# The second layer's expert tiles: the last three of 39 put behind a test of the tile count

## The chip, the cores and the metric

The kernel runs on one core of one Trainium2 chip. The metric is the device time of one execution in microseconds (us). The core has five engines that run side by side, each with its own queue of instructions: TensorE (PE in the profile; its weight loads are PEld), VectorE (DVE), ScalarE (ACT), GpSimd (POOL) and SyncE (SP). A difference of under 0.5% (8 us) is about what a few runs of this kernel cannot tell from none.

## The reference

Two layers work on x, 4 x 512 tokens of 512 numbers in float32. Each layer adds a gated attention and then a gated mixture of experts. The part that the change touches is the mixture of experts of the second layer (`_L1_ffn_ref`), with B*S = 2048 tokens, E = 8 experts of width F = 256, and K = 2 experts for each token:

```python
h = _rmsnorm(x, rms_weight)
ht = h.reshape(-1, d)
logits = ht @ router_w
probs = jax.nn.softmax(logits, axis=-1)
topv, topi = jax.lax.top_k(probs, K)
topv = topv / jnp.sum(topv, axis=-1, keepdims=True)
...
g = jnp.einsum('td,edf->tef', ht, w_gate)
u = jnp.einsum('td,edf->tef', ht, w_up)
eo = jnp.einsum('tef,efd->ted', jax.nn.silu(g) * u, w_down)
moe = jnp.einsum('te,ted->td', w_dense, eo)
sh = jax.nn.silu(ht @ sw_gate) * (ht @ sw_up) @ sw_down
```

`w_dense` holds the two weights of a token in the columns of its two experts. The result, `moe + sh`, is scaled by tanh(g_ffn[1]) and added to x. The inputs are drawn with a fixed seed, so the routing is the same in each run.

## The kernel before

The kernel goes through its stages in order: attention of layer 0, experts of layer 0, attention of layer 1, experts of layer 1. The change is in the last.

**Routing of layer 1** (lines 1806 to 1898). The router's logits give each token its two experts. The tokens of each expert are put one behind the other into *slots*, and each expert's slots begin at a new tile of 128. `cnt` is the number of tiles of each expert (its tokens plus 127, shifted right by 7), and `ends` is the running sum over the experts, so its last column is the number of tiles in use. How many that is depends on the data; at most it is `SLOTS` = (2 * 2048 + 8 * 127) // 128 = 39, and the kernel always works 39 tiles. `idx` holds for each tile the 128 rows of the table to fetch; unused slots point at 128 padding rows behind the 2048 tokens. `owner` is the expert of each tile (for tiles beyond the last in use it is the last expert), and `owners` the same as a one-hot. These are small VectorE operations; between them `advance(besides)` sets the shared expert of the last batch, on TensorE, VectorE and SP.

**The tiles** (`slot_tiles`, line 361, called from line 1923 for layer 1). One tile is:

- `fetch`: POOL starts an indirect DMA that gathers 128 rows of `table1` into `got` (line 368). `got` has depth + 1 = 6 buffers, and `fetch` runs five tiles ahead.
- `turn`: TensorE transposes `got` (4 products, line 379); VectorE scales it into `h_t` (line 383) and makes the tile's weight `wt` (lines 1916, 1917).
- `up`: 8 products with the gate and up weights of the tile's expert (line 397), then Silu on ScalarE (line 406) and a product on VectorE (line 407). The expert's number is read from `owner` into a register of TensorE (line 1907).
- `turn_mid`: 2 transposes (line 413) and a copy on ScalarE (line 415).
- `down`: 4 products with the down weights (line 421), a scaled copy on ScalarE (line 425), and an indirect DMA from POOL that adds the 128 rows to `out` (line 426). Such a scatter waits for the one before it to land.

The loop interleaves these as a pipeline: for each j it issues the fetch of tile j + 5, the middle turn of j - 1, the turn of j + 1, gate and up of j, and down of j - 1. All eight experts' weights are in SBUF before. The order on PE, DVE, ACT and POOL is the one written (`manual_schedule`); no planner moves instructions here.

**The end.** After the last scatter every engine runs a drain and a barrier (line 1997 in the profile). POOL's drain begins behind its last scatter.

**A branch that is there already** (line 1070). In layer 0 each expert has five tiles that always run; more of them, up to sixteen for each expert, stand in a `tc.If` that tests the largest token count, `most`. Each engine loads the value into a register, compares, and either runs the body or jumps behind it, where it updates the semaphores that the body would have updated.

Of the kernel before, what the change touches and what calls it, by code (L numbers as in the profile page):

```python
# [10 lines left out]
FP = mybir.dt.float32  # L11
BF = mybir.dt.bfloat16
I32 = mybir.dt.int32
# [5 lines left out]
P = 128  # L19
B, S, D = 4, 512, 512  # L20
# [16 lines left out]
E1, F1 = 8, 256  # L37
# [2 lines left out]
SLOTS0 = 5  # L40

SLOTS = (2 * B * S + E1 * (P - 1)) // P


WHEN = {'keys': (-7, -6, -5, -3, -2, -1, 0, 2, 3, 4, 5, 6, 7),
# [19 lines left out]
WIDE = D + E1  # L65
# [10 lines left out]
def kernel(  # L76
# [32 lines left out]
    nc = tc.nc  # L109
# [13 lines left out]
    def bank(name):  # L123
        return phase[0].tile([P, 512], FP, tag="bank", bufs=phase[1], name=name)

    def two_banks(name):
        return phase[0].tile([P, 2, 512], FP, tag="two", bufs=2, name=name)
# [31 lines left out]
    table1 = tc.dram_tile([ROWS, WIDE], FP, name="table1")  # L159
# [201 lines left out]
    def slot_tiles(sp, tiles, table, total, width, rms, besides=lambda j: None, depth=3):  # L361

        nf = width // P

        def fetch(j):
            t = tiles[j]
            t.got = sp.tile([P, WIDE], FP, tag="got", bufs=depth + 1, name=f"got_{t.name}")
            nc.gpsimd.indirect_dma_start(  # L368
                out=t.got,
                out_offset=None,  # L370
                in_=table[:, :],
                in_offset=bass.IndirectOffsetOnAxis(ap=t.idx, axis=0),
            )

        def turn(j):
            t = tiles[j]
            tp = bank(f"gotT_{t.name}").rearrange("p (c q) -> p c q", c=NC)
            for c in range(NC):
                nc.tensor.transpose(tp[:, c, :], t.got[:, c * P : (c + 1) * P], ident)  # L379
            t.h_t = sp.tile([P, NC, P], FP, tag="h_t", bufs=2, name=f"h_t_{t.name}")  # L380
            if rms:
                w = cols_sb[:, C_RMS : C_RMS + NC].unsqueeze(2).to_broadcast([P, NC, P])
                nc.vector.tensor_tensor(t.h_t, tp, w, ALU.mult)
            else:
                nc.vector.tensor_copy(t.h_t, tp)  # L385
            t.w = t.scale(t.got[:, D:])

        def up(j):
            t = tiles[j]
            if t.gate_up is None:  # L390
                t.gate_up, t.down = t.weights()
            gu = two_banks(f"gu_{t.name}").rearrange("p k f -> p (k f)")[:, : 2 * width]
            parts = t.gate_up(0)
            n = 2 * width // len(parts)
            for k in range(len(parts)):
                for c in range(NC):
                    nc.tensor.matmul(  # L397
                        gu[:, k * n : (k + 1) * n],
                        lhsT=t.h_t[:, c, :],
                        rhs=t.gate_up(c)[k],  # L400
                        start=(c == 0),
                        stop=(c == NC - 1),
                    )
            act = sp.tile([P, width], FP, tag="slot_act", bufs=2, name=f"act_{t.name}")
            t.mid = sp.tile([P, width], FP, tag="slot_mid", bufs=2, name=f"mid_{t.name}")
            nc.scalar.activation(act, gu[:, :width], AF.Silu)  # L406
            nc.vector.tensor_tensor(t.mid, act, gu[:, width:], ALU.mult)  # L407

        def turn_mid(j):
            t = tiles[j]  # L410
            tp = bank(f"midT_{t.name}")[:, :width].rearrange("p (c q) -> p c q", c=nf)
            for f in range(nf):
                nc.tensor.transpose(tp[:, f, :], t.mid[:, f * P : (f + 1) * P], ident)  # L413
            t.mid_t = sp.tile([P, nf, P], FP, tag="mid_t", bufs=2, name=f"mid_t_{t.name}")
            nc.scalar.copy(t.mid_t, tp)  # L415

        def down(j):
            t = tiles[j]
            py = bank(f"y_{t.name}")
            for f in range(nf):  # L420
                nc.tensor.matmul(  # L421
                    py, lhsT=t.mid_t[:, f, :], rhs=t.down(f), start=(f == 0), stop=(f == nf - 1)
                )
            y = sp.tile([P, D], FP, tag="slot_y", bufs=3, name=f"y_{t.name}")
            nc.scalar.activation(y, py, AF.Copy, scale=t.w)  # L425
            nc.gpsimd.indirect_dma_start(  # L426
                out=total[:, :],
                out_offset=bass.IndirectOffsetOnAxis(ap=t.idx, axis=0),
                in_=y,
                in_offset=None,  # L430
                compute_op=ALU.add,
            )

        n = len(tiles)
        for j in range(depth):
            fetch(j)
        turn(0)
        for j in range(n + 1):
            if j + depth < n:
                fetch(j + depth)  # L440
            if j > 0:
                turn_mid(j - 1)
            if j + 1 < n:
                turn(j + 1)
            if j < n:
                up(j)
                if rms and j + 1 < n:
                    tiles[j + 1].gate_up, tiles[j + 1].down = tiles[j + 1].weights()
                besides(j)
            if j > 0:  # L450
                down(j - 1)
# [68 lines left out]
    with tc.tile_pool(name="att0", bufs=2, reuse_waits="tile") as wk:  # L520
# [9 lines left out]
        for b in range(B):  # L530
            t = Tokens()
# [246 lines left out]
        first, second = logits0(b * TB, 2), logits0(b * TB + 2, 2)  # L778
# [20 lines left out]
        def one_over(s):  # L799
# [3 lines left out]
        dist, fb, zone, rest = wide("dist"), wide("fb"), wide("zone"), wide("rest")  # L803
# [37 lines left out]
            out=table0[: B * S, D:].rearrange("(i p) e -> p i e", p=P), in_=w0  # L841
# [272 lines left out]
    for b in range(B):  # L1114
        nc.sync.dma_start(
            out=x_sb[:, b * TB : (b + 1) * TB, :],
# [8 lines left out]
    with tc.tile_pool(name="att1", bufs=1, reuse_waits="tile") as wk:  # L1125
# [8 lines left out]
        for b in range(B):  # L1134
            t = Batch()
# [486 lines left out]
        with tc.manual_schedule(engines={E.PE, E.DVE, E.Activation, E.Pool}):  # L1622
# [15 lines left out]
            for k, b in itertools.product(WHEN, range(B)):  # L1638
                first = per * b
                f = first - per  # L1640
# [23 lines left out]
                elif k == "shifted":  # L1664
                    for g in range(NC):
                        f = first + g * TB
# [79 lines left out]
    with tc.tile_pool(name="exp1", bufs=1, side="right", reuse_waits="tile") as wk:  # L1746

        wd = wk.tile([P, E1, F1 // P * D], FP, tag="wd", name="wd")
        wgu = wk.tile([P, E1, NC * 2 * F1], FP, tag="wgu", name="wgu")
        idx = wk.tile([P, SLOTS], I32, tag="idx", name="idx")  # L1750
        owner = wk.tile([P, SLOTS], I32, tag="owner", name="owner")
        owners = wk.tile([P, SLOTS, E1], FP, tag="owners", name="owners")
        shp = tc.alloc_tile_pool(name="shared1", bufs=1, side="right", reuse_waits="tile")
        shared1 = []
        for name, src in (("swg", sg1), ("swu", su1), ("swd", sd1)):
            t = shp.tile([P, *((2, 512) if name == "swd" else (4, 256))], FP, tag=name, name=name)
            load_rows(t, src)
            shared1.append(t)
        for t, src in ((wgu, wgu1), (wd, wd1)):
            for e in range(0, E1, 4):  # L1760
                nc.scalar.dma_start(
                    out=t[:, e : e + 4, :], in_=src[e : e + 4].rearrange("e p f -> p e f")
# [43 lines left out]
        with tc.tile_pool(name="route1", bufs=1, reuse_waits="tile") as rp:  # L1806
# [29 lines left out]
            ends = cnt  # L1836
            for k in range(E1.bit_length() - 1):
                t, n = rp.tile([P, E1], FP, tag="ends", bufs=2, name=f"ends{k}"), 1 << k
                nc.vector.tensor_copy(t[:, :n], ends[:, :n])
                nc.vector.tensor_tensor(t[:, n:], ends[:, n:], ends[:, : E1 - n], ALU.add)  # L1840
                ends = t
# [12 lines left out]

            pi = bank("slots")[:, : 2 * SLOTS]
            n = NT // 4
            for h in range(8):
                k, i0 = h // 4, h % 4 * n
                hot_r, hot_c = one_hots(
                    rp, row1[:, k, i0 : i0 + n], col1[:, k, i0 : i0 + n], i0, 0, SLOTS  # L1860
                )
# [9 lines left out]
                if h == 0:  # L1871
# [10 lines left out]
                        out=table1[: B * S, D:].rearrange("(i p) e -> p i e", p=P), in_=w1  # L1882
                    )
            slot_rows(rp, idx, pi)

            ge = rp.tile([P, SLOTS, E1], FP, tag="ge", name="ge")
            own = rp.tile([P, SLOTS], FP, tag="own", name="own")
# [6 lines left out]
            nc.vector.tensor_reduce(own, ge, AX.X, ALU.add)  # L1894
            nc.vector.tensor_scalar(own, own, float(E1 - 1), None, ALU.min)
            nc.vector.tensor_copy(owner, own)
            nc.vector.tensor_scalar(owners[:, :, 0:1], ge[:, :, 0:1], -1.0, 1.0, ALU.mult, ALU.add)
            nc.vector.tensor_tensor(owners[:, :, 1:], ge[:, :, :-1], ge[:, :, 1:], ALU.subtract)
            for k in range(12):
# [3 lines left out]
        def slots1(pool, j):  # L1903
            gate_up, down = (w.rearrange("p e f -> p (e f)") for w in (wgu, wd))

            def weights():
                e = nc.tensor.value_load(owner[0:1, j : j + 1], min_val=0, max_val=E1 - 1)
                n = 2 * F1
                return (
                    lambda c: (gate_up[:, bass.ds(e * (NC * n) + c * n, n)],),  # L1910
                    lambda f: down[:, bass.ds(e * (F1 // P * D) + f * D, D)],
                )

            def scale(w):
                t = pool.tile([P, E1 + 1], FP, tag="wt", bufs=4, name=f"wt_{j}")
                nc.vector.tensor_tensor(t[:, :E1], w, owners[:, j, :], ALU.mult)
                nc.vector.tensor_reduce(t[:, E1:], t[:, :E1], AX.X, ALU.add)
                return t[:, E1:]

            return Slots(f"s1_{j}", idx[:, j : j + 1], weights, scale)  # L1920

        with tc.tile_pool(name="slots1", bufs=1, reuse_waits="tile") as sp:
            slot_tiles(sp, [slots1(sp, j) for j in range(SLOTS)], table1, out, F1, True, depth=5)
    layer1.close()
    close_psum()

# [74 lines left out]
```

## Time and profile before

| what | us |
|---|---|
| three timed runs | 1603.37, 1610.71, 1612.19 |
| their median | 1610.71 |
| the profiled execution | 1603.29 |
| span of its trace, first to last instruction | 1601.5 |
| TensorE busy in the span | 1462.0 (91%) |
| layer 1's tiles: first gather issued | 1353.5 |
| first gate-and-up product | 1360.2 |
| last scatter issued | 1593.8 |
| one gather on POOL (79 of both layers) | 0.99 |
| one scatter into `out` on POOL (39) | 1.59 |
| such a scatter, issue to landing | 4.5 to 5.0 |
| granted TensorE clock, mean over the span | 0.963 |

A line of the groups reads: line, engine, operation, output <- inputs, count, busy time, mean of one in ns, and the idle time before them with what ended it. The chain is the sequence of work that ended last, followed back from the last instruction; its lines are start, length, engine and line. In a table by stretch each pair is the busy time of an engine and its number of instructions, and "PEclk" is the share of the full TensorE clock that was granted. A `q` behind an engine's name (POOLq) marks what its sequencer does, such as register loads, branches and drains.

### The profile page before, as it was taken

To read this page: it belongs to the slowest core of one execution; us is meant where nothing else is said; L and a number is where in the kernel's file an instruction comes from. 1 tells how busy PE (TensorE), PEld (TensorE's weight loads), DVE (VectorE), ACT (ScalarE), POOL (GpSimd) and SP (SyncE) were. 2 spreads that over 40 slices of the span, in tenths; PEclk is the share of its full clock that TensorE was granted. 3 is DMA by queue.
4 is the path that set the end of the run, shared out by engine and by line. 5 is a ranking of instruction groups with operands and counts; after the bars stand their busy time and mean duration, and the time that the engine had idled before them with its cause. 6 is when DMAs were issued, how large, how long until landed. Compare 5 with 4: busy or idle time off the path is not lost.

```text
span 1601.5 us, 14963 instructions
## 1 busy us (share of the span) xinstructions
PE 1462.0 (91%) x5558; PEld 648.0 (40%) x5558; DVE 643.7 (40%) x1167; ACT 474.9 (30%) x683; POOL 576.9 (36%) x454
## 2 busy tenths in 40 slices
PE   7999699999999999897878989987799987999997
PEld 3553244444444444442222332332334353445443
DVE  4755222232221211254575566556654346222221
ACT  3653111112111111333454444444434210122221
POOL 0000112213132222225458566676476411344442
PEclk9999899999999999997999999999799988999998
DMA  9414224533433422500000000000000147344453
GB/s 324 124 72 165 65 42 117 132 92 73 125 93 79 119 53 35 176 11 4 0 1 1 1 0 14 27 1 1 27 27 27 53 182 283 75 90 91 91 93 46
DMA packets 60751, 121.42 MB, mean 76 GB/s; under 512 B 10496, under 2 KB 13056, under 8 KB 59648
## 3 DMA queue, kind: packets, MB, share of 16 engines
q0 software_dynamic: 17696, 41.75, 14.1%
q1 hardware_dynamic: 35872, 64.86, 11.6%
q10 hardware_dynamic: 7104, 13.78, 2.3%
q8 instruction: 47, 0.77, 0.2%
q14 instruction: 32, 0.26, 0.1%
HBM read 81.70 MB, written 38.67 MB: 75 GB/s over the span
## 4 chain that ended last, share of the span: by engine, by line
PE 66%; DVE 7%; POOL 6%; ACT 4%; issue 3%; DMA 2%; POOLq 0%; ACTq 0%; SPq 0%; DVEq 0%
PE gu_s L397 26%; PE y_s L421 13%; DVE nm L1448 4%; PE sc L1431 4%; PE m L1431 4%; ACT pt L1481 4%; PE q L1170 2%; PE y L1170 2%; PE gotT_s L379 2%; PE gu L1170 2%; PE midT_s L413 2%; PE o L1499 2%; POOL acc L1489 2%; POOL xln L1240 1%; POOL acc L1486 1%
## 5 line engine op out<-in xcount | busy, mean ns | idle before, releaser
L368 POOL DMA_INDIRECT got_s<-table,idx x79 | 77.9, 986 | 567.5 <-ACT y_s L425 324.4
L421 PE MATMUL y_s<-wd,mid_t_s 128*128 128x512 f32 (+1 forms) x476 | 218.6, 595 | 1.6 <-ACT mid_t_s L415 1.6
L1448 DVE TENSOR_REDUCE nm<-m 128x4 f32<-128x1984 f32 x64 | 142.3, 2223 | 166.6 <-PE m L1431 166.6
L407 DVE TENSOR_TENSOR mid_s<-act_s,gu_s 128x512 f32<-128x512 f32 (+1 forms) x79 | 43.9, 555 | 393.1 <-ACT act_s L406 393.1
L1481 ACT ACTIVATE pt<-sc 128x2048 f32<-128x2048 f32 x64 | 120.2, 1878 | 191.9 <-PE sc L1431 174.3
L1489 POOL TENSOR_TENSOR acc<-acc,pt 128x2048 f32<-128x2048 f32 (+1 forms) x32 | 144.3, 4509 | 64.9 <-ACT pt L1481 64.9
L406 ACT ACTIVATE act_s<-gu_s 128x512 f32<-128x512 f32 (+1 forms) x79 | 38.9, 492 | 392.7 <-PE gu_s L397 392.6
L397 PE MATMUL gu_s<-wg,h_t_s 128*128 128x512 f32 x320 | 145.1, 596 | 0.0
L397 PE MATMUL gu_s<-wu,h_t_s 128*128 128x512 f32 x320 | 143.9, 592 | 0.0
L397 PE MATMUL gu_s<-wgu,h_t_s 128*128 x312 | 142.7, 601 | 0.0
L421 PEld LDWEIGHTS y_s<-wd,mid_t_s 128*128 128x128 f32 x476 | 89.2, 190 | 112.7 <-issue 107.5
L1431 PE MATMUL sc<-xT,k_t 32*128 32x512 f32 (+1 forms) x512 | 78.6, 685 | 34.6 <-DVE nm L1448 33.3
L1486 POOL TENSOR_TENSOR acc<-pt,pt 128x2048 f32<-128x2048 f32 x16 | 72.2, 4511 | 102.6 <-ACT pt L1481 102.6
L426 POOL DMA_INDIRECT out<-y_s,idx x39 | 61.8, 1584 | 130.2 <-ACT mid_t_s L415 122.7
L1431 PE MATMUL m<-k_t,xT 32*128 32x496 f32 x512 | 74.5, 653 | 23.8 <-ACT pt L1481 17.0
L397 PEld LDWEIGHTS gu_s<-wu,h_t_s 128*128 128x128 f32 x320 | 60.8, 190 | 76.5 <-issue 76.5
L397 PEld LDWEIGHTS gu_s<-wg,h_t_s 128*128 128x128 f32 x320 | 58.2, 192 | 58.3 <-issue 57.9
L397 PEld LDWEIGHTS gu_s<-wgu,h_t_s 128*128 128x128 f32 x312 | 57.1, 193 | 57.6 <-issue 57.6
L426 POOL DMA_INDIRECT sum<-y_s,idx x40 | 63.5, 1586 | 42.6 <-ACT y_s L425 27.1
L1499 PE MATMUL o<-pt,v 128*32 128x512 f32 (+1 forms) x512 | 72.9, 644 | 0.0
L425 ACT ACTIVATE y_s<-y_s,got_s 128x512 f32<-128x512 f32 x40 | 27.5, 687 | 122.5 <-PE y_s L421 122.5
L385 DVE COPY h_t_s<-gotT_s 128x512 f32<-128x512 f32 x40 | 27.6, 690 | 87.4 <-PE gotT_s L379 87.4
(361 smaller groups left out, 2010.9 us busy)
## 6 DMA issues: line engine op xcount, KB each, us to landing
wg<-in_wg SPq DMA_DIRECT2D x8, 1024.0 KB, 7.4
wu<-in_wu SPq DMA_DIRECT2D x8, 1024.0 KB, 7.0
wd<-in_wd SPq DMA_DIRECT2D x8, 1024.0 KB, 5.7
table<-xln SPq DMA_DIRECT2D x32, 256.0 KB, 2.0
wgu<-in_wgu ACTq DMA_DIRECT2D x2, 4096.0 KB, 15.6
ctx<-in_ctx_t SPq DMA_DIRECT2D x8, 512.0 KB, 10.4
x_sb<-in_x SPq DMA_DIRECT2D x4, 1024.0 KB, 13.8
sum<-x_sb SPq DMA_DIRECT2D x16, 256.0 KB, 2.0
```

The source lines that it names most:

```text
L368: nc.gpsimd.indirect_dma_start(out=t.got, out_offset=None, in_=table[:, :], in_offset=bass.IndirectOffsetOnAxis(ap=t.idx, axis=0),)
L397: nc.tensor.matmul(gu[:, k * n : (k + 1) * n], lhsT=t.h_t[:, c, :], rhs=t.gate_up(c)[k], start=(c == 0), stop=(c == NC - 1),)
L407: nc.vector.tensor_tensor(t.mid, act, gu[:, width:], ALU.mult)
L421: nc.tensor.matmul(py, lhsT=t.mid_t[:, f, :], rhs=t.down(f), start=(f == 0), stop=(f == nf - 1))
L426: nc.gpsimd.indirect_dma_start(out=total[:, :], out_offset=bass.IndirectOffsetOnAxis(ap=t.idx, axis=0), in_=y, in_offset=None, compute_op= ...
L1170: nc.tensor.matmul(pp, lhsT=lhs(c), rhs=w[:, c, :], start=(c == 0), stop=(c == n - 1))
L1431: nc.tensor.matmul(sc[:n, j, :width], lhsT=lhs(rs), rhs=rhs(rs), start=True, stop=True)
L1448: nc.vector.tensor_reduce(it.nm[g][:, t, :], sc[:, :, :S2], AX.X, ALU.max, negate=True)
L1481: nc.scalar.activation(it.pt[:n], sc[:n], AF.Exp)
L1486: nc.gpsimd.tensor_tensor(acc, it.pt0, it.pt, ALU.add)
L1489: nc.gpsimd.tensor_tensor(acc[:n], acc[:n], it.pt[:n], ALU.add)
L1499: nc.tensor.matmul(it.po[j * HD : (j + 1) * HD, :], lhsT=it.v[:n, c, h * HD : (h + 1) * HD], rhs=pt[:n, j, :], start=(c == 0), stop=(c == ...
```

## The change

The tiles of layer 1 are worked in two calls of `slot_tiles`: one for tiles 0 to `USUAL` - 1, with `USUAL` = (2 * 2048 + 8 * 128 // 2) // 128, and one for the tiles from there to `SLOTS` - 1. The second call stands in a `tc.If`, whose condition is that the number of tiles in use is greater than `USUAL`. That number is copied as an integer into a new tile `total` by one VectorE cast in the routing, and `values_load` reads it into a register on every engine. The second call has a pipeline of its own, with a depth of three, and begins after the first has issued its last scatter. The number of `got` buffers, which was depth + 1, is now given outright: 6 in layer 1 and 4 in layer 0, as before.

```diff
+USUAL = (2 * B * S + E1 * P // 2) // P
...
-            t.got = sp.tile([P, WIDE], FP, tag="got", bufs=depth + 1, name=f"got_{t.name}")
+            t.got = sp.tile([P, WIDE], FP, tag="got", bufs=6 if rms else 4, name=f"got_{t.name}")
...
+        total = wk.tile([P, 1], I32, tag="total", name="total")
...
             nc.vector.tensor_copy(owner, own)
+            nc.vector.tensor_copy(total, ends[:, E1 - 1 :])
             nc.vector.tensor_scalar(owners[:, :, 0:1], ge[:, :, 0:1], -1.0, 1.0, ALU.mult, ALU.add)
...
         with tc.tile_pool(name="slots1", bufs=1, reuse_waits="tile") as sp:
-            slot_tiles(sp, [slots1(sp, j) for j in range(SLOTS)], table1, out, F1, True, depth=5)
+            for first, end in ((0, USUAL), (USUAL, SLOTS)):
+                with ExitStack() as rest:
+                    if first > 0:
+                        used = nc.values_load(total[0:1, 0:1], min_val=0, max_val=SLOTS)
+                        rest.enter_context(tc.If(used > USUAL))
+                    slot_tiles(
+                        sp,
+                        [slots1(sp, j) for j in range(first, end)],
+                        table1,
+                        out,
+                        F1,
+                        True,
+                        depth=min(5, end - first),
+                    )
```

## The prediction

> **What bounds the kernel now.** I read the page first, for who is busy; then the chain that ended last, cut to the last 47 us, for how the second layer's slot tiles follow each other; then the sums by stretch, to see whether TensorE has any slack there; then the one place where the kernel already branches, for the price of a branch.
>
> The page (busy time by engine, and the chain by line):
>
> ```profile
> PE 1462.0 (91%) x5558; PEld 648.0 (40%) x5558; DVE 643.7 (40%) x1167; ACT 474.9 (30%) x683; POOL 576.9 (36%) x454
> PE gu_s L397 26%; PE y_s L421 13%; DVE nm L1448 4%; PE sc L1431 4%; PE m L1431 4%; ACT pt L1481 4%; PE q L1170 2%; PE y L1170 2%; PE gotT_s L379 2%; PE gu L1170 2%; PE midT_s L413 2%; PE o L1499 2%; POOL acc L1489 2%; POOL xln L1240 1%; POOL acc L1486 1%
> ```
>
> The chain at the end (start, length, what):
>
> ```profile
> 1571.22 3.44 PE gu_s L397 x8
> 1574.66 1.72 PE y_s L421 x4
> 1576.37 0.22 PE midT_s L413 x2
> 1576.59 0.44 PE gotT_s L379 x4
> 1577.03 3.44 PE gu_s L397 x8
> 1580.46 1.72 PE y_s L421 x4
> 1582.18 0.22 PE midT_s L413 x2
> 1582.40 3.44 PE gu_s L397 x8
> ...
> 1588.55 4.51 DMA out<-y_s,idx
> ...
> 1593.59 1.79 POOLq L1997
> ```
>
> Every tile is one turn of the same wheel on TensorE: 3.44 (gate and up) + 1.72 (down, of the tile before) + 0.22 + 0.44 (two turns) = 5.82 us; start to start, 1571.22 to 1577.03, it is 5.81. The last tile's turn is shorter (1577.03 to 1582.40, 5.37), as no tile behind it is turned. What follows is a tail: activation, product, the last y, the scatter of tile 37 landing, then that of tile 38.
>
> By stretch (length, then busy time of PE, PEld, DVE, ACT, POOL, granted clock, DMA share, GB/s), three turns in the middle and the last three full ones:
>
> ```profile
> 1397.89:1415.32 17.43, 17.43 (x55) 8.67 (x54) 4.04 (x13) 4.00 (x9) 7.73 (x7) 1.00 0.50 92
> 1565.25:1582.68 17.43, 17.43 (x54) 8.44 (x53) 4.04 (x12) 4.00 (x10) 4.67 (x3) 1.00 0.34 46
> ```
>
> TensorE is busy for all 17.43 us at full clock, no other engine for half of it. Here time goes with the number of tiles.
>
> **Does the test skip the tiles?** USUAL is (4096 + 8*64) // 128 = 36, and the body runs if the tiles in use exceed 36. The count is the sum over experts of tokens/128, rounded up. I worked out the second layer's router from the reference for the drawn inputs: 274, 456, 223, 1058, 896, 207, 769, 213 tokens, so 3+4+2+9+7+2+7+2 = 36. 36 > 36 is false: tiles 36 to 38, which hold only padding, are jumped over. It is exact: expert 4 fills seven tiles to the last row (896 = 7*128), and one more token makes 37. The closest single change of choice that does so needs a logit gap of 0.0076 to close (expert 4 third behind a second that loses no tile); the logits computed in single and in double precision differ by 5e-5 at most. With random errors of 0.003 on every logit 12 of 200 draws gave 37, with 0.001 none.
>
> **What is removed.** Tiles 36, 37, 38. The built programs' order is the same on all engines up to tile 30's scatter, but for one DVE cast and a few register instructions on SP; from there tiles 34 and 35 get the ending that 37 and 38 had, the same instructions with the same kinds of waits. So the old tail hangs on an earlier turn: gate and up of the last-but-one tile started at 1577.03; in the new kernel that is tile 34, which three turns of 5.81 earlier is at 1559.60. Gain 17.43 us. It contains 3 x (8+4+2+4) TensorE products with three register operations for each tile, and, off the path, 3 gathers (986 ns) and 3 scatters (1587 ns) of POOL, 3 x (0.69+0.16+0.16+0.42) of DVE and 3 x (0.38+0.36+0.69) of ACT, all worth nothing by themselves. The two exceptions to the wheel, its opening (clock at half, see below) and its tail, stay whole.
>
> **What is added, early.** A cast of one column, `total<-ends`, on DVE between `owner` and `owners`. Nearest row: the cast to `owner`, 128x39, 0.18 us. DVE ends its routing with a residual at 1355.13 and waits until 1357.66 for the first turned tile: 2.5 us of cover, so 0. Without cover it would be 0.18. SP loads the register (0.49 + 0.19 + 0.04 by SP's records of L1070) ahead of its last store of `out`; the register's value is there at about 1354.2, the store's source at 1355.1, so at most 0.1 us, and its first reader is the first scatter at 1374: 0. SP issues nothing after it.
>
> **What is added, at the end.** Each engine loads `total` and branches after its last instruction of tile 35. The kernel has one such jump already, over the spare tiles of layer 0, of which the trace has none (L1070; min/median/max ns, first and last start):
>
> ```profile
> L1070 POOLq TENSOR_LOAD <-most x1: 546/546/546, 164.2 to 164.2; - x1
> L1070 POOLq COMPARE_BRANCH  x1: 45/45/45, 164.9 to 164.9; - x1
> L1070 POOLq EVENT_SEMAPHORE  x4: 17/42/43, 167.6 to 167.9; - x4
> L1070 POOLq INC_SWDGE_SEM  x1: 176/176/176, 168.0 to 168.0; - x1
> L1070 PEldq COMPARE_BRANCH  x1: 3379/3379/3379, 174.5 to 174.5; - x1
> ```
>
> Load 0.55, compare 0.05, then 2.7 us until POOL's next instruction; DVE 3.0 (175.7 to 178.8), ACT 2.65 (177.0 to 179.7), PE 3.4. [...]
>
> Does it lie on the path? Let T be the dispatch of the last scatter; in the new kernel T = 1593.81 - 17.43 = 1576.38. PE is done at T - 3.2 and would be past a jump at T + 0.7; ACT (last y ends at T - 2.5) also at T + 0.7. POOL's sequencer runs ahead of its scatter (the DRAIN below starts at 1593.59, before the scatter's own 1593.81), so POOL reads at T - 0.2, is past the jump at T + 3.2, past four waits and the semaphore update at T + 3.8. The waits there are for transfers older than tile 35's scatter. That scatter lands at T + 4.67 (1598.48 in the trace). Until then all of it is hidden, by 0.9 us on POOL and by 4 us elsewhere.
>
> What ends the kernel is POOL's drain (7065 ns, from 1593.6 to 1600.66, 2.2 us after the landing):
>
> ```profile
> L1997 POOLq DRAIN  x3: 46/113/7065, 1593.6 to 1601.2; - x3
> ```
>
> If it ends by the landing, as ACT's DRAIN ends with ACT's last work (1591.33 and 1591.30), the later start costs 0. If it took 7.07 us from its own start, T + 3.8, it would end at T + 10.9 for T + 6.85: 4.0 us. A gain has no mechanism beyond the 17.43. I take 0.3, near the first, since the drain's end follows the landing.
>
> **Sum.** 17.43 - 0.3 = 17.1 us. The profiled execution took 1603.29, 1.8 more than its span: 1586.2 for its like. The three timed runs were 1603.37, 1610.71, 1612.19; the profiled one sits with the fastest. From the median 1610.71: 1593.6.
>
> **Rivals.**
> 1. *The body runs* (37 tiles on the chip). Then POOL gathers tile 36 only after the scatter of 35 and the load: about 1578.3, lands 3.4 later (first gather 1353.49, landed 1356.93) at 1581.7. PE has idled since 1573.1, 8.5 us. In the opening of this stage PE went from first landing to the second tile's gate and up in 10.9 us (1356.93 to 1367.80), with the clock at half after a smaller gap:
>
> ```profile
> 1360.24:1364.64 4.40, 4.40 (x7) 1.82 (x7) 0.92 (x3) 0.00 (x0) 1.55 (x2) 0.50 0.65 197
> ```
>
> [...] Second-to-last tile at 1592.6, plus the tail 1577.03 to 1601.5 (24.47): 1617.1, 15.6 slower: 1626. It decides from one token more in expert 4. Against it: the count above.
> 2. *The end costs more than I see*: the drain starts over, or POOL's jump waits for the scatter: gain 13.4, 1597.3. For it: no row shows a drain that starts late.
> 3. *The end eats over 9.4 us*, so that the change is within 0.5%: about 1603. It would take a jump three times as long as the four seen.
>
> **How the numbers follow.** Forecast 0.82 (1593.6; its own range, from the two levels of the runs, 1585 to 1596), rival 2 0.09, rival 3 0.04, rival 1 0.05. Differences under 0.5% (8 us) are about what the runs, 0.55% apart, can't tell from none. Faster: the forecast but for 0.02 of scatter, and rival 2: 0.89; same 0.05; slower 0.06. Range 1583 to 1600: the lower level less 17.4 and 0.2%, and 1612.2 - 13.4 = 1598.8, rounded up.
>
> **What would show it.** Right: no line for gathers after tile 35 (36 gathers and 36 scatters in layer two), gate-and-up products x288 for x312, turns still 5.81, the last scatter near 1576.4 and the span near 1584. Each engine has a load of `total` and a compare. If POOL's drain ends more than 2.2 us after the last landing, the tail's price was wrong; if 39 scatters are there, the count was.

## The result, and the profile after

| | before | after |
|---|---|---|
| median, 11 runs each | 1606.8 us (1603.37 to 1613.75) | 1590.64 us (1583.89 to 1601.22) |
| ratio, with its 95% interval | | 0.990 (0.9874 to 0.9925) |
| profiled execution | 1603.29 | 1593.11 |
| its span | 1601.5 | 1590.8 |
| layer 1's first gather issued | 1353.49 | 1359.79 |
| first gather to the end of the span | 248.01 | 230.99 |
| last scatter issued | 1593.81 | 1583.33 |

The changed kernel is 1% faster: 16.2 us by the medians, 12.1 to 20.2 by the interval (0.0075 and 0.0126 of 1606.8). The two spans differ by 10.7 us only. The stage with the tiles is 17.02 us shorter, but in this pair of executions it began 6.30 us later. (10.7 is 17.0 less 6.3.)

The page after, busy time by engine, and from the groups the two whose counts tell how many tiles ran (count | busy, mean ns | idle before):

```profile
span 1590.8 us, 14804 instructions
PE 1453.3 (91%) x5504; PEld 643.2 (40%) x5504; DVE 640.2 (40%) x1156; ACT 471.4 (30%) x674; POOL 569.8 (36%) x448
...
L399 PE MATMUL gu_s<-wgu,h_t_s 128*128 x288 | 131.6, 600 | 0.0
...
L428 POOL DMA_INDIRECT out<-y_s,idx x36 | 57.0, 1584 | 121.9 <-ACT mid_t_s L417 111.9
```

288 gate-and-up products are 36 tiles of 8, and there are 36 scatters. POOL has 6 instructions fewer (three gathers, three scatters), TensorE 54 (three tiles of 18). The tiles that hold only padding did not run.

The chain that ended last, its second half, as shown of before:

```profile
1559.86 3.44 PE gu_s L399 x8
1563.30 1.72 PE y_s L423 x4
1565.01 0.22 PE midT_s L415 x2
1565.23 0.44 PE gotT_s L381 x4
1565.67 3.44 PE gu_s L399 x8
...
1576.81 0.37 ACT mid_t_s L417
1577.19 0.90 issue
1578.08 4.49 DMA out<-y_s,idx
...
1583.12 0.33 POOLq L1930
1583.45 1.43 POOL out L428
```

One turn is 5.81 us, as before (1559.86 to 1565.67). The order at the end is as before too: tile 34's scatter lands, then tile 35's is issued. New are 0.90 us of "issue" ahead of tile 34's scatter, and POOL's register load (L1930).

The table by stretch shows both stages whole (length, then busy time and count of PE, PEld, DVE, ACT, POOL, granted clock, DMA share, GB/s), and ahead of it 35 us of layer 1's attention at the same place in both. After:

```profile
780.00:815.00 35.00, 25.33 (x141) 7.19 (x142) 16.88 (x14) 16.84 (x16) 21.53 (x14) 0.80 0.00 0
...
1359.79:1590.78 230.99, 212.69 (x648) 104.91 (x648) 50.12 (x151) 48.15 (x108) 92.58 (x72) 0.97 0.45 84
```

Before:

```profile
780.00:815.00 35.00, 26.13 (x170) 9.40 (x170) 19.89 (x14) 15.26 (x16) 24.69 (x14) 0.90 0.00 0
1353.49:1601.50 248.01, 230.22 (x702) 113.66 (x702) 54.09 (x162) 52.09 (x117) 100.14 (x78) 0.97 0.46 85
```

In the stage with the tiles the granted clock is 0.97 in both, so its two lengths can be compared. In the attention 0.80 was granted in the execution after, 0.90 in that before. Over its 11 runs the changed kernel's time follows the mean granted clock (1583.89 us at 0.964, 1601.22 at 0.949; correlation -0.93). Most of the 6.3 us arose in this attention: VectorE's reduction that starts at 748.57 in the execution before starts 2.0 us later in that after (750.56), and the one at 899.68 starts 6.3 us later (906.00). The change's early additions do not hold the first gather up: other kernels below that have them issued it at 1352.80 and 1355.03. From here on I compare by *stretch*, first gather to end of span, and by the timed ratio beside it.

Within the stretch: first gather to first gate-and-up product went from 6.75 to 6.81; from there to the start of the last gate-and-up product from 225.00 to 207.28, which is 17.72 less; from there to the last scatter from 8.57 to 9.45; from there to the end from 7.70 to 7.45. Together (+0.06 - 17.72 + 0.88 - 0.25) 17.03 less.

### The profile page after: what moved, and what is told of

Read it like the earlier page. It is cut to its first block, busy times and chain, and to the rows that moved or that the text cites. A ratio compares the mean times of both kernels' runs of the same rounds, so it can differ in the third digit from the quotient of the medians.

```text
span 1590.8 us, 14804 instructions
## 1 busy us (share of the span) xinstructions
PE 1453.3 (91%) x5504; PEld 643.2 (40%) x5504; DVE 640.2 (40%) x1156; ACT 471.4 (30%) x674; POOL 569.8 (36%) x448
## 4 chain that ended last, share of the span: by engine, by line
PE 66%; DVE 6%; POOL 6%; ACT 4%; issue 3%; DMA 2%; POOLq 0%; ACTq 0%; SPq 0%; DVEq 0%
PE gu_s L399 25%; PE y_s L423 13%; DVE nm L1450 4%; PE sc L1433 4%; PE m L1433 4%; ACT pt L1483 3%; PE q L1172 3%; PE y L1172 2%; PE gotT_s L381 2%; POOL acc L1491 2%; PE gu L1172 2%; PE o L1501 2%; PE midT_s L415 2%; POOL xln L1242 1%; POOL acc L1488 1%
## 5 line engine op out<-in xcount | busy, mean ns | idle before, releaser
L423 PE MATMUL y_s<-wd,mid_t_s 128*128 128x512 f32 (+1 forms) x464 | 212.9, 595 | 1.6 <-ACT mid_t_s L417 1.6
L399 PE MATMUL gu_s<-wgu,h_t_s 128*128 x288 | 131.6, 600 | 0.0
L428 POOL DMA_INDIRECT out<-y_s,idx x36 | 57.0, 1584 | 121.9 <-ACT mid_t_s L417 111.9
L399 PEld LDWEIGHTS gu_s<-wgu,h_t_s 128*128 128x128 f32 x288 | 52.7, 193 | 53.1 <-issue 53.1
```

The source lines that it names most:

```text
L399: nc.tensor.matmul(gu[:, k * n : (k + 1) * n], lhsT=t.h_t[:, c, :], rhs=t.gate_up(c)[k], start=(c == 0), stop=(c == NC - 1),)
L423: nc.tensor.matmul(py, lhsT=t.mid_t[:, f, :], rhs=t.down(f), start=(f == 0), stop=(f == nf - 1))
L428: nc.gpsimd.indirect_dma_start(out=total[:, :], out_offset=bass.IndirectOffsetOnAxis(ap=t.idx, axis=0), in_=y, in_offset=None, compute_op= ...
```

## The experiments

My theory: the gain is three turns of TensorE, and the test at the end costs nothing, as it lies beside the last scatter's landing. Against it stood three doubts: the jump is on the path after all; the drain takes longer when it starts late; what a run of the body costs was only estimated. Everything by stretch in one table:

| kernel | first gather | last scatter after it | span's end after that | stretch | ratio to before (95%) |
|---|---|---|---|---|---|
| before | 1353.49 | 240.32 | 7.7 | 248.0 | |
| after | 1359.79 | 223.54 | 7.5 | 231.0 | 0.990 (0.9874 to 0.9925) |
| e1_again | 1363.12 | 224.00 | 7.6 | 231.6 | 0.9904 (0.9872 to 0.9937) |
| e2_fixed36 | 1352.06 | 224.00 | 7.4 | 231.4 | 0.9915 (0.9885 to 0.9945) |
| e6_if_only | 1358.80 | 239.99 | 7.5 | 247.5 | 1.0005 (0.9981 to 1.0028) |
| e3_body_runs | 1355.03 | | | 262.0 | 1.0116 (1.0078 to 1.0155) |
| e8_fetched_ahead | 1358.81 | | | 251.2 | 1.0009 (0.9994 to 1.0024) |
| e9_ahead_not_run | 1352.80 | 224.01 | 7.8 | 231.8 | 0.9912 (0.9885 to 0.9939) |
| e4_far | 1368.12 | 224.37 | 9.4 | 233.8 | 0.9917 (0.9879 to 0.9954) |
| e5_three_far | 1355.69 | 224.36 | 18.1 | 242.5 | 0.9978 (0.9959 to 0.9996) |
| e7_four_more | 1359.73 | 223.39 | 7.8 | 231.2 | 0.9883 (0.9846 to 0.992) |

The two executions of the changed kernel itself are 0.6 us apart in their stretches, so smaller differences between single stretches are not read as effects.

### The gain without the branch, and the branch without the gain

e1_again is the changed kernel, run beside the next two.

> The changed kernel as it is, once more, beside the others on one chip. By the theory (three turns of 5.81 us less, the branch under cover) the stretch from the second layer's first gather to the end of the span is 231.0 us within 0.5, as in the first profile (230.99), against 248.0 of the kernel before, whatever the whole span is; timed, 0.99 of the kernel before within 0.004. If the 0.90 us by which the scatter of tile 34 left late in the first profile belongs to the branch, it is there again; if it was chance, the stretch is 230.1.

e2_fixed36 works 36 tiles with no test at all. (It leaves out tiles 36 to 38 whatever the routing, so it fits only routings of up to 36 tiles.)

```diff
-            slot_tiles(sp, [slots1(sp, j) for j in range(SLOTS)], table1, out, F1, True, depth=5)
+            slot_tiles(sp, [slots1(sp, j) for j in range(36)], table1, out, F1, True, depth=5)
```

(against the kernel before)

> The kernel before with 36 tiles written into the loop and no test, no copy of the count and no branch; it works only routings that need no more than 36 tiles. If the branch costs nothing, the stretch from the first gather to the end is within 1 us of that of the changed kernel (230 to 231), and the times are the same within 0.3%. If the branch eats a part of the gain (the rival: POOL's drain starts over behind the jump), this one is faster by up to 4 us: a stretch of 227.

e6_if_only works all 39 tiles and then has a body that can never run.

```diff
-            for first, end in ((0, USUAL), (USUAL, SLOTS)):
+            for first, end in ((0, SLOTS), (USUAL, SLOTS)):
...
-                        rest.enter_context(tc.If(used > USUAL))
+                        rest.enter_context(tc.If(used > SLOTS))
```

> One part alone: all 39 tiles run unconditionally, and behind them stands the branch, never taken into its body (the count is tested against 39). The cost of the added parts without what they save. By the theory 248.0 us within 1 for the stretch and the time of the kernel before within 0.3%; by the rival of the drain that starts over 252.

Measured: stretch 231.6 with the test (231.0 in the first profile), 231.4 without, and the ratios 0.9904 and 0.9915. The test as a whole costs less than these executions differ. The drain begins later with it and ends where it would have: e2_fixed36's drain takes 6784 ns, e1_again's 5304, and both end 1.93 us after the last landing. POOL's load of `total` ahead of the last scatter doesn't hold that scatter up either: it leaves 0.75 us after the landing that it waits for, in e1_again as in e2_fixed36.

e6_if_only gives no difference from before (1.0005), but it shows less than I meant it to. Its trace has neither a load of `total` nor a compare on TensorE, VectorE, ScalarE or POOL, only SP's load and the semaphore updates. With 39 given as the largest value, `used > 39` can't be true, so the test was probably settled when the program was built. So it shows that the cast, SP's load and the updates are free; that loads and compares are free rests on e2_fixed36 against the changed kernel.

### The other side: the body runs

e3_body_runs moves the test by one, so that 36 tiles are enough to enter the body and its three tiles of padding run.

```diff
-                        rest.enter_context(tc.If(used > USUAL))
+                        rest.enter_context(tc.If(used > USUAL - 1))
```

> The changed kernel with the test at 35 in place of 36, so that the body, three tiles of padding, is run. The rival of the prediction priced this case at 15.6 us over the kernel before: TensorE idles from the end of tile 35 until tile 36's gather lands, some 8.5 us, and the next eight gate-and-up products run at half the clock (5.9 us for 3.4). Expected: a stretch of 263 to 264 us against 248.0, 1.01 of the kernel before. If fetching and filling were hidden, 248 to 250.

e8_fetched_ahead enters the body too, but the gathers for its tiles are issued in the first call's pipeline, ahead of the test.

```diff
-    def slot_tiles(sp, tiles, table, total, width, rms, besides=lambda j: None, depth=3):
+    def slot_tiles(sp, tiles, table, total, width, rms, besides=lambda j: None, depth=3, later=()):
...
-            t = tiles[j]
+            t = [*tiles, *later][j]
+            if t.got is not None:
+                return
...
-            if j + depth < n:
+            if j + depth < n + len(later):
...
+            every = [slots1(sp, j) for j in range(SLOTS)]
...
-                        rest.enter_context(tc.If(used > USUAL))
+                        rest.enter_context(tc.If(used > USUAL - 1))
...
-                        [slots1(sp, j) for j in range(first, end)],
+                        every[first:end],
...
+                        later=every[end:],
```

> The test at 35, so that the three tiles of padding are run, with their gathers issued in the first call's loop, ahead of the branch, instead of behind it. In the run with the gathers behind the branch TensorE idled 10.2 us and its next products ran at 0.83 of the clock; the stretch was 262.0. If the gather behind the branch is what makes the body dear, the idle time falls to under 1.5 us and the stretch to 251 to 253, 3 to 5 us over the kernel before. If the branch itself or the refilled pipeline is, it stays above 257.

Measured: 262.0 and 251.2, that is 14.0 and 3.1 us more than before. The timeline of TensorE around the jump (start, length, what; in brackets the idle time and what ended it), e3_body_runs:

```profile
1572.50 1.98 PE L423 MATMUL y_s<-wd,mid_t_s 128*128 x4 [0.82 <-ACT mid_t_s L417]
1584.72 1.94 PE L381 MATMUL gotT_s<-ident,got_s 128*128 128x128 f32 x8 [10.23 <-DMA got_s<-table,idx]
1586.59 4.28 PE L399 MATMUL gu_s<-wgu,h_t_s 128*128 x8
```

and e8_fetched_ahead:

```profile
1576.62 1.98 PE L425 MATMUL y_s<-wd,mid_t_s 128*128 x4 [0.82 <-ACT mid_t_s L419]
1578.44 1.04 PE L383 MATMUL gotT_s<-ident,got_s 128*128 128x128 f32 x8
1579.82 3.70 PE L401 MATMUL gu_s<-wgu,h_t_s 128*128 x8 [0.35 <-DVE h_t_s L387]
```

In e3_body_runs TensorE waits 10.23 us for a gather which only the entered body issues. In that idle time, which begins at 1574.5, the granted clock falls to half from about 1577.7, and it is back some 3 us after TensorE has started again (the third number from the right is the granted clock):

```profile
1575.00:1577.50 2.50, 0.00 (x0) 0.00 (x0) 0.00 (x0) 0.21 (x1) 0.00 (x0) 1.00 0.76 105
1577.70:1587.70 10.00, 2.98 (x10) 2.16 (x11) 1.76 (x6) 0.00 (x0) 4.50 (x4) 0.50 0.48 108
1587.90:1592.50 4.60, 3.62 (x13) 1.61 (x12) 0.42 (x1) 0.50 (x2) 0.00 (x0) 1.00 0.00 0
```

So the wait also makes the work behind it longer, by 1.5 us: the eight transposes took 1.94 us for 1.04 in e8_fetched_ahead, the eight products 4.28 for 3.70. With the gather issued before, the wait and the slow clock are gone (TensorE idles 0.98 us at most there, and the eight products take 3.70 us, for 3.60 at a full clock), and 10.8 of the 14.0 us with them. What makes the body dear is the load behind the test, not the test: here the compare is passed and not jumped, and with the data at hand TensorE goes on at once (the transposes at 1578.44 had no idle time ahead of them). Of the 3.1 us that stay, 2.15 are idle time of TensorE at the seam of the two pipelines (0.82, 0.35 and 0.98 us).

e9_ahead_not_run is the same with the change's own test, so the three gathers are issued and their tiles skipped.

```diff
-                        rest.enter_context(tc.If(used > USUAL - 1))
+                        rest.enter_context(tc.If(used > USUAL))
```

(against e8_fetched_ahead)

> The same with the test at 36, so that the tiles are fetched and not worked. Three gathers of POOL more than in the changed kernel, in its idle time: 0 us. As POOL's count of transfers ahead of the last scatters is then that of the kernel before, the late one falls on the scatter of tile 32 and the stretch is 230.1 to 230.4, 0.6 to 1.2 under the changed kernel; timed, 0.99 of the kernel before, the same as the changed kernel within 0.3%.

Measured: stretch 231.8, ratio 0.9912. The shorter end that I expected did not come: one scatter left late earlier (tile 32's, 0.95 us after its data were there), but so did the next ones (0.72, 0.97). Those had to wait for the one before them: they left 0.82 and 0.75 us after its landing, and with 4.8 to 4.9 us for a landing such a chain takes 5.6 us for each tile, hardly less than the 5.81 of a turn. So a late scatter delayed those behind it here. The three gathers ahead of the test cost nothing that shows. This version is as fast as the changed kernel where the tiles are skipped, and 11 us better than it where they run.

### What a jump costs when its target is far

e4_far puts 400 small instructions for POOL into the body that is jumped over, so that POOL's target lies further on.

```diff
+                    if first > 0:
+                        spare = sp.tile([P, 2], FP, tag="spare", name=f"spare_{first}")
+                        for k in range(400):
+                            nc.gpsimd.memset(spare[:, 0:1], 0.0)
```

> The changed kernel with 400 fills of one column on POOL at the end of the body that is jumped over, so that POOL's jump goes further; nothing of it runs. In the first profile of the change POOL went on 0.14 us after its compare, where over layer 0's body it had taken 2.7. If distance is what makes a jump dear, it is 2 to 3 us here. The cover (the last scatter lands 4.7 us after it is issued) still holds then, and the end does not move: stretch 231.0 within 0.7. If POOL's jump is on the path, 233 to 234.

e5_three_far has three such bodies one behind the other, each with its own load and test, all skipped.

```diff
-            for first, end in ((0, USUAL), (USUAL, SLOTS)):
+            for first, end in ((0, USUAL), (USUAL, SLOTS), (USUAL, SLOTS), (USUAL, SLOTS)):
```

(and the lines of e4_far)

> The same far body and its test three times in a row, all jumped over. POOL needs about 3 x (0.33 load + 0.06 compare + 2.7 jump + 0.5 semaphores) = 10.8 us from the dispatch of the last scatter, and the cover ends after 4.7. By the theory the end now moves: POOL's drain begins some 10.6 us after the last scatter instead of 1.4, and the span ends 4 to 5 us later, stretch 235 to 236. If jumps are short at any distance, 231 to 232.

What POOL's sequencer did at the test and at the end (ns as minimum, median, maximum, then first and last start), the changed kernel:

```profile
L1928 POOLq EVENT_SEMAPHORE  x3: 17/43/43, 1583.7 to 1583.9; - x3
...
L1928 POOLq COMPARE_BRANCH  x1: 58/58/58, 1583.5 to 1583.5; - x1
L1928 POOLq INC_SWDGE_SEM  x1: 745/745/745, 1584.0 to 1584.0; - x1
```

```profile
L2014 POOLq DRAIN  x3: 46/113/5192, 1584.7 to 1590.5; - x3
```

and e4_far:

```profile
L1928 POOLq EVENT_SEMAPHORE  x4: 17/30/43, 1595.5 to 1597.9; - x4
...
L1928 POOLq COMPARE_BRANCH  x1: 58/58/58, 1592.7 to 1592.7; - x1
L1928 POOLq INC_SWDGE_SEM  x1: 734/734/734, 1598.0 to 1598.0; - x1
```

```profile
L2018 POOLq DRAIN  x3: 46/107/2315, 1598.7 to 1601.6; - x3
```

In the changed kernel the first of the waits starts 0.14 us after the compare's end, and the drain begins 1.4 us after the last scatter was issued. In e4_far 2.7 us pass between the compare's end and the first wait, then the waits themselves stretch over 2.4 us (a second stall, 1595.66 to 1597.88), the update takes 0.73, and the drain begins 6.25 us after the last scatter was issued (1592.49), 1.3 us after it had landed (1597.40). The DMA view of these microseconds (1592.0 to 1599.0) shows what went on in the stalls:

```profile
q14 instruction: 3, 0.02, 1.1%
```

Three packets of instructions were fetched, one within each of the two stalls and one while the update ran; in the changed kernel this queue has none from 1575 to 1586, which takes in its jump. So e4_far measured the reading that I had not favoured for it: the cover did not hold. It is 4.9 us long here and the way past the jump 6.25. The end of the kernel came 9.4 us after the last scatter instead of 7.5, 1.9 us more. The rest of the longer stretch lies ahead of the last scatter, where no jump is. The timed ratio, 0.9917, can't tell 1.9 us.

The late drain also shows how long it takes with nothing left to wait for: 2.3 us here, neither the 7.07 of before nor zero. e5_three_far confirms it and gives the price of a pass:

```profile
L1928 POOLq COMPARE_BRANCH  x3: 45/45/58, 1580.2 to 1591.5; - x3
L1928 POOLq INC_SWDGE_SEM  x3: 714/721/739, 1586.1 to 1594.3; - x3
```

```profile
L2018 POOLq DRAIN  x3: 46/107/2315, 1595.0 to 1597.9; - x3
```

Last scatter at 1580.05, landed by 1584.95, drain from 1595.04: three passes took 15.0 us, and the drain 2315 ns again. The end came 18.1 us after the last scatter, 10.7 more than in the changed kernel. I had the direction and less than half of the size. The first pass stalled twice, as in e4_far (2.5 and 3.0 us), and took 6.8 us; the second and the third stalled once each (2.7 and 2.5) and took 4.2 and 3.9. Each of these four stalls has one packet of instructions within it. I had counted one stall for each pass, 0.5 us for the waits and the update together, where the update alone takes 0.72, and nothing for the drain's own 2.3. By time it is 0.9978: three far jumps give back most of what the skipped tiles bring.

### The late scatter

In the changed kernel tile 34's scatter was issued 1.17 us after its data were ready, not 0.28 as its neighbours. It is not the branch: in e2_fixed36, which has none, the wait before the last-but-one scatter is as long. POOL's timeline there:

```profile
1564.56 1.55 POOL L426 DMA_INDIRECT out<-y_s,idx  x1 [4.25 <-ACT mid_t_s L415]
1570.78 1.55 POOL L426 DMA_INDIRECT out<-y_s,idx  x1 [4.66 <-ACT mid_t_s L415]
1576.06 1.55 POOL L426 DMA_INDIRECT out<-y_s,idx  x1 [3.73 <-DMA out<-y_s,idx]
```

(From 1564.56 to 1570.78 it is 6.22 us where a turn has 5.81.) In the runs of the changed kernel and in e2_fixed36 it was always the 151st indirect transfer of POOL; in before the late one was the 152nd, tile 32's scatter, which left 0.77 us after its data where nothing hung on it. To see whether the place decides, e7_four_more issues four more gathers, of rows that nobody reads, early in the stage.

```diff
+            if rms and n == USUAL and j in (6, 7, 8, 9):
+                more = sp.tile([P, WIDE], FP, tag="more", bufs=4, name=f"more_{j}")
+                nc.gpsimd.indirect_dma_start(
+                    out=more,
+                    out_offset=None,
+                    in_=table[:, :],
+                    in_offset=bass.IndirectOffsetOnAxis(ap=tiles[j].idx, axis=0),
+                )
```

> The changed kernel with four more gathers on POOL (rows of tiles 6 to 9 once more, into buffers that nothing reads), issued early in the stage, where POOL idles 3 us in every turn. In all profiles so far one of POOL's indirect transfers left 0.6 to 1.5 us late at about the same place in its own count (the 114th, and the 151st or 152nd), with 36 tiles on the last-but-one scatter, whether there is a branch or not, and with 39 tiles on the scatter of tile 32, where the pipeline hides it. If the place in the count decides, the four more move the late one to the scatter of tile 32 or 33, the scatter of tile 34 leaves 0.28 us after its y, and the stretch is 230.1 to 230.4 instead of 231.0 to 231.6. If the place in the tail decides, the scatter of tile 34 is late again and the stretch is 231 to 231.6.

Measured: the late one is now tile 31's scatter (0.81), and tile 34's comes 0.43 after its data; a similar late one moved from tile 13 to tile 11. So the place in POOL's count of transfers (the 152nd here too) decides which one is late. What happens at that place no run shows. The gain that this should have brought is not there: the last scatter comes 223.4 us after the first gather (223.5 to 224.4 in the others with 36 tiles), and the end 7.8 after it, not 7.5. The stretch is 231.2, among the others. What tile 34's scatter won by leaving sooner, 0.74 us, was lost beside it: it took 4.87 us to land, for 4.49 in the chain of the changed kernel:

```profile
1577.33 0.16 issue
1577.49 4.87 DMA out<-y_s,idx
```

The last scatter took 4.84 us to land for 4.67, and the products up to there took 0.41 us longer. Why a landing takes 4.5 us in one execution and 4.9 in another is not shown.

## Why the prediction was right, and where it was not

1. *The count, and what is removed.* 36 tiles, three turns of 5.81: the products from first to last gate and up took 17.72 us less, for 17.43 predicted. The 0.29 between them lies within what executions differ by: in e1_again the products took 17.29 us less than before, in e2_fixed36 17.04. The count is exactly 36 on the chip, as the body is skipped by a test at 36 and entered by one at 35 (e3_body_runs). That the turns are the whole of the gain is shown from both sides: 36 tiles without the test give it (e2_fixed36), and the test's additions to 39 tiles give nothing (e6_if_only, as far as it goes).

2. *The early additions at 0.* Right. SP's load began at 1360.4, and its last store was issued at 1361.52, 1.72 us after the first gather, for 1.67 before; the first scatter of the stage is some 20 us later. First gather to first product changed by 0.06.

3. *The jumps, at 2.7 us on POOL as at L1070.* This step was wrong, and the sum survived it because the cover was there. From compare to the next instruction it was 0.14 us on POOL (1583.59 to 1583.73), 0.17 on VectorE and at most 0.30 on ScalarE, where the row of L1070 gave 2.7, 3.0 and 2.65. On TensorE the compare took 0.36, for 3.4 of the row. Its next instruction came at 1579.26, 1.13 later, but its own last product had run until 1579.21, so that no time of a jump shows there. (ScalarE's 0.30 too ends with its own last activation.) On POOL the compare alone was 58 ns, and 198 ns with the gap behind it. e4_far shows the dear case: with 400 instructions more in the skipped body the 0.14 became 2.7, with a fetch on the instruction queue within it. The body here has three tiles, that of L1070 eleven for each of eight experts, and I had taken the row of the far jump for the near one.

4. *The other small terms.* The load took 0.30 to 0.33 us, not 0.55; the semaphore update of POOL 0.745, not 0.176. POOL's drain thus began 1.4 us after the last scatter's issue where I had 3.8.

5. *"Until then all of it is hidden, by 0.9 us on POOL".* The conclusion held with more room than I gave it: 4.67 us of landing against 1.4. But my own dear figures had left out a term. With the far jump (e4_far) the way was 6.25 us and not 3.8, because among the four waits behind the jump came a second stall of 2.2, and the update took 0.73. The trace of before had that stall already: behind the jump of L1070 POOL stood still once more, from 168.24 to 170.09, with one packet of instructions in that time. Where the row does apply, in e4_far, 1.9 us were lost, and not 0.3.

6. *The drain.* "If it ends by the landing, the later start costs 0" was the right branch: it ends 1.93 us after the landing (2.18 before; 1.9 to 2.2 in all runs), whenever it starts before that. But it wasn't free when late: 2.3 us from its own start (e4_far, e5_three_far). The 7.07 from its own start, which rival 2 needed, was the other end of the bracket and did not occur.

7. *The tail, 0.3.* Measured +0.88 up to the last scatter and -0.25 behind it. The 0.88 comes from the late scatter of tile 34, which I had not foreseen; with the products' 0.29 more and 0.06 at the opening the net loss is 0.40 (17.43 less 17.03). That the total is within 0.1 of 17.1 is partly this cancelling. "Last scatter near 1576.4" and "span near 1584" missed by the stage's later start: with 6.30 added to 1576.38 it would be 1582.68, and it was 1583.33.

8. *The level.* 1593.6 was built on the median of three, 1610.71; over 11 runs before has 1606.8, and less 17.1 that is 1589.7, for 1590.64. The profile that I summed against lay among the faster executions of before (clock 0.963), that of after among the middle ones of its own (0.959).

9. *The rivals.* Rival 1's mechanism is real (a gather that waits for the branch), and its price was 14.0, not 15.6. TensorE's idle time was 10.23 us for my 8.5, but the restart was cheaper than the opening that I took it from: from the gather's landing to the last-but-one tile's gate and up 8.0 us (1584.58 to 1592.56) for 10.9. The clock did fall to half, some 3 us after TensorE had stopped (from 1574.5 to 1577.7), and came back some 3 us after its restart (from 1584.7 to 1587.7). But the transposes of two tiles took up most of the slow stretch, and only its last 1.2 us fell on the eight products, which took 4.28 us, for 3.70 in e8_fetched_ahead and 5.92 in the opening. So the slow clock cost 0.6 us in the products and 0.9 in the transposes. Rival 3's price needs three far jumps in a row (e5_three_far, 10.7 us), not one.

## What to carry to other kernels

Here a test that skips three turns of the bound engine brought those turns (17.0 us of the stretch), as the load, the compare and the jump lay behind the last instruction of their engine and beside a transfer that had to land anyway (1.4 us on POOL beside 4.67). Where you put such a test, write down how long that cover is for each engine, above all for the one whose drain ends the kernel. The price of a jump is read from one of the same length: from the compare to the end of POOL's update it was 1.2 us here where the target is near, and 3.6 to 6.6 where it is far. And let the loads of a conditional body be issued ahead of its test, if a buffer is free: here three gathers that are wasted cost nothing that shows (a stretch of 231.8 us, for 231.0 and 231.6 of the changed kernel), and a body that does run cost 3.1 us instead of 14.0.

## What the runs showed of the hardware that I had not expected

- A far jump stalled POOL for 2.5 to 2.7 us (e4_far, e5_three_far), and in the first of a row once more a few instructions on, for 2.2 and 3.0 us. One packet of instructions was fetched within each stall.
- POOL's drain took 2.3 us where it began after the last landing (2315 ns in e4_far and e5_three_far, begun 1.3 and 10 us after it); begun earlier, it ended 1.9 to 2.2 us after the landing.
- POOL's update of its transfer semaphore took 0.71 to 0.88 us behind the scatters of this stage, and 0.18 at the jump in layer 0.
- Some indirect transfers of POOL started 0.4 to 1.2 us late, in these runs at the same places in its count (the 114th, the 151st or 152nd), whatever tile fell there. The cause is open.
- The clock at half behind an idle of 10.2 us of TensorE cost about 1.5 us in the work that followed, as it was back some 3 us after the restart.
